# Stores moved to GpSimd's queue, a new reading order for PSUM banks, and a new order of work after the last image in a two-layer spectral kernel

## The chip, the cores and the metric

The kernel runs on one core of one Trainium2 chip. The metric is the device time of one execution in microseconds (us). A core has a matrix engine (TensorE, PE in the profile), a vector engine (VectorE, DVE), a scalar engine (ScalarE, ACT), a general engine (GpSimd, POOL) and a queue processor (SyncE, SP). TensorE writes its results to PSUM (eight banks), from which DVE and ACT read them. DMA transfers between main memory and the on-chip SBUF are issued in order from the queues of SP, ACT or POOL. All matrix work here is in 32-bit floating point.

## What is computed

The input `x` has 32 images of 32 channels, each channel a 128 x 128 matrix. Two layers follow each other, each on a normalised copy of its input (`_gn`: mean and variance over two channels):

```python
def _L0_conv_ref(A):                 # five Newton-Schulz steps towards the matrix square root
    normA = jnp.sqrt(jnp.sum(A2 * A2, axis=(1, 2)))
    Y = A2 / normA[:, None, None];  Z = I
    for _ in range(5):
        T = 0.5 * (3.0 * I - Z @ Y);  Y = Y @ T;  Z = T @ Z
    return Y * jnp.sqrt(normA)[:, None, None]
def _L1_conv_ref(x, weights1, weights2):       # a spectral layer on 2 x 32 x 32 modes
    x_dht = fftn(x).real
    top = einsum('bixy,ioxy->boxy', x_dht[:, :, :32, :32], weights1)
    bot = einsum('bixy,ioxy->boxy', x_dht[:, :, -32:, :32], weights2)
    return ifftn(out_dht).real                 # out_dht holds top and bot, zero elsewhere
x = x + _L0_conv_ref(_gn(x))
x = x + _L1_conv_ref(_gn(x), weights1, weights2)
```

## The kernel before

**Layer 0** works on groups of four channels, 8 groups to an image, 256 in all. `fetch` loads a group, `staged` scales it (four tensor_scalar on POOL at line 272, the sum with a scaled identity at line 291), and `newton` runs its chain of matrix products: TensorE multiplies (lines 248 and 254), DVE evicts some results (line 242) and ACT others (lines 234 and 236), POOL adds the identity in the middle of the chain (line 315), and DVE adds the result to the input tile `xt` (line 326). Four groups, the `lanes`, run interleaved, so that TensorE has another group's products while one waits for an eviction. Before an image's first group `prep` loads the whole image (`xs`, line 167) and takes its statistics on DVE (`bn_stats`, line 175).

**Between the layers** each finished group goes through `settle`: a copy of `xt` to main memory (`mid`, line 335), two sums of its column halves on POOL (`fold`, line 340), and `bn_stats` (line 344). After four groups `forward` transforms the folds (lines 358 to 370), and after eight `spectrum` makes the image's 64 x 32 modes (line 395), waits for the statistics (lines 147 to 155, 413 to 432), scales the modes and stores them (`xs`, line 449).

**Layer 1** works on sets of images, `GROUPS = (21, 8, 3)`. Once a set's last spectrum is stored, its products with the weights run (`wide_products`, line 492, for the first set; `small_products`, line 556, for the others), the results go to main memory (`od`), and then each image of the set goes through `inverse`. An inverse loads the products (`ob` or `or`, line 590) and the image's copy (`yt`, four tiles of 8 channels, line 601), transforms in two steps (lines 644 and 666), copies the sine half from PSUM to `d` on ACT (line 675), adds the cosine half from PSUM to `yt` on DVE (line 681), adds and subtracts `d` on POOL (`unfold`, line 619), and stores the result (`store`, line 609).

**The order.** The program is a set of generators. A round goes over the four lanes; queues named `preps`, `specs`, `posts`, `prods` and `backs` are stepped at fixed lanes, so that one round does one step of `posts` (folds and forwards), one of `specs` (spectra) and so on:

```python
if i == 2: step(specs)
if i == 3: step(posts)
if i == 0 or tail: step(prods)
if i == 0 and rounds % 5 or tail: step(backs)
```

`tail` is true when no group of layer 0 is left. Inverses of the second set (images 21 to 28) are left over then, and those of the third (29 to 31) can't begin, since image 31 is in that set. Once the tail has no `posts` left, the SBUF of layer 0 (`sets`) is freed and a pool `late` takes it: there go the weights of the last products (`wt_late`, 14 loads of 512 KB on POOL's queue, line 779) and three zeroed tiles (`xk_late`, line 776).

A scheduler fixes each engine's order when the program is built; the calls in `kept(...)` stay in program order among themselves on their queue. Every engine and every queue then works strictly in its order: an instruction that waits for a semaphore holds up everything behind it. The copies, loads of `xs` and `yt`, and stores of results all go through SP's queue, except that in the tail `store` uses ACT's.

Of the kernel before, what the change touches and what calls it, by code (L numbers as in the profile page):

```python
# [24 lines left out]
F32 = mybir.dt.float32  # L25
# [6 lines left out]
P = 128  # L32
B = 32
# [26 lines left out]
def conv_preact_kernel(  # L60
# [8 lines left out]
    nc = tc.nc  # L69
# [20 lines left out]
    mid = [dram.tile([P, C, P], F32, name=f"mid{b}", tag=f"mid{b}") for b in range(B)]  # L90
# [16 lines left out]
    inv = ctx.enter_context(tc.tile_pool(name="inv", bufs=1))  # L107
# [10 lines left out]
    tail = False  # L118

    def page(name):  # L120
        return modes.tile([P, 1024], F32, tag="page", name=name, bufs=3)

    def bank():
        return ps8.tile([P, 4, P], F32, tag="ps", name="ps")
# [33 lines left out]
    kept = tc.keep_in_program_order  # L158
# [173 lines left out]

    def settle(b, g, st, xt):

        kept(nc.sync.dma_start(out=mid[b][:, 4 * g : 4 * g + 4, :], in_=xt))
        if g % 2 == 0:
            folds[b, g // 2] = sets.tile([P, 8, P], F32, tag="fold", name=f"fold{b}_{g}", bufs=3)
        f = folds[b, g // 2][:, 4 * (g % 2) : 4 * (g % 2) + 4, :]
        for half, op in enumerate((ALU.add, ALU.subtract)):
            nc.gpsimd.tensor_tensor(  # L340
                f[:, :, 64 * half : 64 * half + 64], xt[:, :, 0:64], xt[:, :, 64:128], op
            )
        for j in range(4):
            nc.vector.bn_stats(st[:, 4 * g + j, :], xt[:, j, :])
        yield
# [110 lines left out]
    def wide_products(i):  # L456
# [26 lines left out]
        for step in range(2 * KK):  # L483
# [23 lines left out]
            if step + 2 < 2 * KK:  # L507
                load(step + 2)
        store(*done)
        yield  # L510

# [65 lines left out]
    yts = {}  # L577

    def load_products(b):
        if b < B and b not in obs:  # L580
            g, n = where[b]
            few = GROUPS[g] <= NB

            ob = page(f"or{b}") if few else inv.tile([P, 1024], F32, tag="ob", name=f"ob{b}", bufs=2)
            if few:
                src, dst = od[g][:, :, :, n, :].rearrange("k q l x -> (k q) l x"), "p (l x) -> p l x"
            else:
                src, dst = od[g][:, :, n, :].rearrange("k q x -> (k q) x"), "p (l x) -> p (l x)"
            for e in range(2):
                kept(nc.sync.dma_start(out=ob[64 * e : 64 * e + 64].rearrange(dst, l=4), in_=src))  # L590
            obs[b] = ob

    def load_input(b, e):

        if b >= B or (b, e) in yts:
            return
        yts[b, e] = []
        for i in range(2):
            o = 16 * e + 8 * i
            y = inv.tile([P, 8, P], F32, tag="yt", name=f"yt{b}_{o}", bufs=6)  # L600
            kept(nc.sync.dma_start(out=y, in_=mid[b][:, o : o + 8, :]))  # L601
            yts[b, e].append(y)

# [2 lines left out]
    def store():  # L606
        while stores:
            b, o, y = stores.pop(0)
            kept((nc.scalar if tail else nc.sync).dma_start(out=out[b, :, o : o + 8, :], in_=y))  # L609

    sums = []

    def unfold():

        while sums:
            b, o, y, d = sums.pop(0)
            for half, op in enumerate((ALU.subtract, ALU.add)):
                yh = y[:, :, 64 * half : 64 * half + 64]
                nc.gpsimd.tensor_tensor(yh, yh, d, op)  # L619
            stores.append((b, o, y))  # L620

    def inverse(b):


        more = where[b][1] < GROUPS[where[b][0]] - 1
        load_products(b)
        load_input(b, 0)
        yield
        ob = obs[b]
        if GROUPS[where[b][0]] <= NB:  # L630
            ob = inv.tile([P, 1024], F32, tag="ob", name=f"ob{b}", bufs=2)
            nc.scalar.copy(  # L632
                ob.rearrange("p (o t l) -> p o t l", t=8, l=4),
                obs[b].rearrange("p (l t o) -> p o t l", l=4, t=8),
            )
        ob = ob.rearrange("p (e j m) -> p e j m", e=2, j=4)
        if more:
            load_products(b + 1)

        pg = [bank() for _ in range(2)]  # L640
        for j in range(4):
            for e in range(2):
                rows = slice(64 * e, 64 * e + 64)
                nc.tensor.matmul(
                    pg[e][:, j, :], ob[rows, e, j, :], tab[rows, T_IH], start=True, stop=True
                )
        gts = []
        for e in range(2):
            gts.append(inv.tile([P, 4, P], F32, tag="gt", name=f"gt{b}_{e}", bufs=3))
            nc.scalar.copy(gts[e], pg[e])  # L650
        unfold()
        yield
        for e in range(2):
            store()

            py = [bank().rearrange("p j x -> p (j x)") for _ in range(4)]
            py = [p.rearrange("p (s c h) -> p s c h", s=2, h=64) for p in py]
            cos, sin = (slice(T_IW.start + P * i, T_IW.start + P * i + P) for i in range(2))
            for s, table, h, g in (
                (0, cos, slice(0, 64), slice(0, 64)),  # L660
                (1, sin, slice(1, 64), slice(65, 128)),
                (1, cos, slice(0, 1), slice(64, 65)),
            ):
                for i in range(4):
                    rows = slice(32 * i, 32 * i + 32)
                    nc.tensor.matmul(
                        py[i][:, s, :, h],
                        tab[rows, table],
                        gts[e][rows, :, g],
                        start=True,  # L670
                        stop=True,
                    )
            d = page(f"d{b}_{e}").rearrange("p (c h) -> p c h", h=64)
            for i in range(4):
                nc.scalar.copy(d[:, 4 * i : 4 * i + 4, :], py[i][:, 1])  # L675
            for i in range(2):
                for j in range(2):
                    y = yts[b, e][i][:, 4 * j : 4 * j + 4, :]
                    y = y.rearrange("p c (s h) -> p c s h", s=2)
                    half = py[2 * i + j][:, 0, :, None, :].to_broadcast([P, 4, 2, 64])  # L680
                    nc.vector.tensor_tensor(y, half, y, ALU.add)  # L681
                unfold()
                sums.append((b, 16 * e + 8 * i, yts[b, e][i], d[:, 8 * i : 8 * i + 8, :]))
                if not i:
                    yield
            if not e:
                load_input(b, 1)
            elif more:
                load_input(b + 1, 0)
            yield  # L690
        if not more:
            unfold()
            yield
            store()
# [3 lines left out]
    posts = []  # L698
    specs = []
# [3 lines left out]
    def step(queue):  # L703
        if queue and next(queue[0], queue) is queue:
            queue.pop(0)


    late = []
    late_xks, late_wts = [], []
# [6 lines left out]
    ended = {}  # L716
# [50 lines left out]
    rounds = 0  # L767
    while todo or any(lanes) or posts or specs or prods or backs:
        tail = not todo and not any(lanes)
        if tail and not posts and not late:  # L770

            phase.close()
            late.append(ctx.enter_context(tc.tile_pool(name="late", bufs=1)))
            for i in range(3):
                late_xks.append(late[0].tile([P, 4 * NB, 64], F32, name=f"xk{i}_late"))
                nc.gpsimd.memset(late_xks[-1], 0.0)
            for kk in range(2, KK):
                late_wts.append(late[0].tile([P, 2, 4, 4, C], F32, name=f"wt{kk}_late"))
                nc.gpsimd.dma_start(out=late_wts[-1], in_=wk[kk])
        for i in range(LANES):  # L780
            if lanes[i] is None and todo and rounds >= 3 * i:
                b, g = todo.pop(0)
                xt = ready[0][0]
                lanes[i] = (b, g, xt, newton(g, made[b][2], *ready.pop(0)))
                if stages:
                    stage()
            if lanes[i] is not None:
                b, g, xt, steps = lanes[i]
                if next(steps, lanes) is lanes:
                    lanes[i] = None  # L790
                    end(b, g, xt)
            if i == 1:
                step(preps)
            if i == 2:
                step(specs)
            if i == 3:
                step(posts)
            if i == 0 or tail:
                step(prods)
            if i == 0 and rounds % 5 or tail:  # L800
                step(backs)
        rounds += 1

# [63 lines left out]
```

## Time and profile before

Three runs took 3258.66, 3259.20 and 3259.95 us; the profiled execution has a span of 3256.9 us. Times below are counted from the span's start.

| stretch, us | what runs | PE busy | DVE busy | POOL busy | data moved |
|---|---|---|---|---|---|
| 100 to 1960 | layer 0 alone | 1841.35 of 1860.00 | 1361.42 | 940.20 | 98 GB/s |
| 1960 to 3105.6 | layer 0, with layer 1 of earlier images beside it | 1103.67 of 1145.60 | 806.60 | 724.57 | 214 GB/s |
| 3105.6 to 3256.9 | the tail: what is left of layer 1 | 60.91 of 151.30 | 36.43 | 73.76 | 267 GB/s |

A stretch in which PE is busy all the time can only get shorter by less matrix work; one in which it is idle has another cause for its length, and the chain of waits has to be followed there. The times at which the tail's stages begin:

| event in the tail | start, us |
|---|---|
| last `xt` added up (line 326), ends | 3105.6 |
| last forward's first matmul (line 358) | 3109.29 |
| last image's spectrum on PE (line 395) | 3141.35 |
| its store to main memory (line 449) | 3163.15 |
| first product of the third set (line 556) | 3173.65 |
| first `ob` copy of the third set's inverses (line 632) | 3208.77 |
| first result of image 29 issued for storing (line 609) | 3221.41 |
| end | 3256.9 |

### The profile page before, as it was taken

To read this page: it belongs to the slowest core of one execution; us is meant where nothing else is said; L and a number is where in the kernel's file an instruction comes from. 1 tells how busy PE (TensorE), PEld (TensorE's weight loads), DVE (VectorE), ACT (ScalarE), POOL (GpSimd) and SP (SyncE) were. 2 spreads that over 40 slices of the span, in tenths; PEclk is the share of its full clock that TensorE was granted. 3 is DMA by queue.
4 is the path that set the end of the run, shared out by engine and by line. 5 is a ranking of instruction groups with operands and counts; after the bars stand their busy time and mean duration, and the time that the engine had idled before them with its cause. 6 is when DMAs were issued, how large, how long until landed. Compare 5 with 4: busy or idle time off the path is not lost. (4 is left out here: it accounts for less than half of the span.)

```text
span 3256.9 us, 78280 instructions
## 1 busy us (share of the span) xinstructions
PE 3076.2 (94%) x30656; PEld 2944.7 (90%) x30656; DVE 2265.8 (70%) x6372; ACT 1457.9 (45%) x3068; POOL 1784.7 (55%) x2333
## 2 busy tenths in 40 slices
PE   6999999999999999999999999999999999999944
PEld 6999999999999999999999999899989898989933
DVE  5777777777777777777777776477777776756631
ACT  3444444444444444444444444444444444435522
POOL 4554545455454545444555554367667766746663
PEclk9999999999999999999999999999999999999966
DMA  3333333332233333333322336676666666686596
GB/s 121 98 104 98 101 101 102 95 97 93 88 102 101 102 101 98 104 98 95 95 90 93 101 98 194 210 223 208 227 218 196 208 224 220 215 263 191 186 319 208
DMA packets 271746, 479.37 MB, mean 147 GB/s; under 512 B 80656, under 2 KB 91408, under 8 KB 271376
## 3 DMA queue, kind: packets, MB, share of 16 engines
q1 hardware_dynamic: 191744, 318.61, 30.7%
q10 hardware_dynamic: 77616, 148.41, 14.1%
q0 software_dynamic: 2016, 7.34, 0.6%
q8 instruction: 242, 3.96, 0.5%
q14 instruction: 128, 1.05, 0.1%
HBM read 319.06 MB, written 155.19 MB: 146 GB/s over the span
## 5 line engine op out<-in xcount | busy, mean ns | idle before, releaser
L340 POOL TENSOR_TENSOR fold<-xt 128x256 f32<-128x256 f32 x512 | 362.6, 729 | 645.4 <-DVE xt L326 581.0
L291 POOL TENSOR_TENSOR r<-b,eye 128x512 f32<-128x512 f32 x256 | 326.6, 1276 | 609.1 <-issue 584.5
L248 PE MATMUL ps<-w,v 128*128 128x128 f32 x4096 | 548.1, 277 | 4.7 <-DVE w L242 3.2
L248 PE MATMUL ps<-y,q 128*128 128x128 f32 x4096 | 544.2, 276 | 1.2 <-ACT y L234 1.2
L248 PEld LDWEIGHTS ps<-w,v 128*128 128x128 f32 x4096 | 500.1, 193 | 7.8 <-DVE w L242 4.6
L248 PEld LDWEIGHTS ps<-y,q 128*128 128x128 f32 x4096 | 500.3, 193 | 2.1 <-ACT y L234 1.6
L234 ACT COPY y<-ps 128x512 f32<-128x512 f32 x512 | 299.5, 585 | 361.9 <-PE ps L248 361.7
L272 POOL TENSOR_SCALAR x<-xt,a_nm,a_sc 128x128 f32<-128x128 f32 x1024 | 448.3, 451 | 21.9 <-DVE a_n L204 20.1
L282 ACT ACTIVATE b<-b,a_off,a_scr 128x128 f32<-128x128 f32 x1024 | 422.3, 486 | 1.9 <-DMA b<-in_x 1.8
L619 POOL TENSOR_TENSOR yt<-yt,d 128x512 f32<-128x512 f32 x256 | 319.4, 1274 | 164.7 <-DVE yt L681 151.1
L242 DVE SCALAR_TENSOR_TENSOR w<-ps,r 128x512 f32<-128x512 f32 x512 | 347.3, 683 | 56.3 <-PE ps L254 53.5
L242 DVE SCALAR_TENSOR_TENSOR q<-ps,eye 128x512 f32<-128x512 f32 x512 | 348.9, 683 | 51.6 <-PE ps L248 43.2
L175 DVE BATCH_NORM_STATS2 a_st<-xs 128x6 f32<-128x128 f32 x1024 | 231.5, 280 | 216.8 <-DMA xs<-in_xt 215.8
L315 POOL TENSOR_TENSOR r<-mb,eye 128x512 f32<-128x512 f32 x256 | 325.7, 1272 | 23.1 <-ACT mb L236 23.1
L236 ACT ACTIVATE mb<-ps 128x512 f32<-128x512 f32 x256 | 153.1, 598 | 408.1 <-PE ps L254 407.0
L254 PE MATMUL ps<-ident,v 128*128 128x128 f32 x2048 | 312.3, 275 | 13.9 <-DVE v L242 13.3
L242 DVE SCALAR_TENSOR_TENSOR v<-ps,m 128x512 f32<-128x512 f32 x256 | 175.6, 686 | 213.1 <-PE ps L248 212.3
L326 DVE SCALAR_TENSOR_TENSOR xt<-ps,a_t_s,xt 128x128 f32<-128x128 f32 x1024 | 289.2, 342 | 49.5 <-PE ps L248 47.9
L248 PE MATMUL ps<-m,q 128*128 128x128 f32 x2048 | 283.6, 282 | 31.7 <-DVE q L242 30.8
L248 PEld LDWEIGHTS ps<-m,q 128*128 128x128 f32 x2048 | 250.2, 193 | 46.1 <-DVE q L242 31.8
L248 PE MATMUL ps<-y,t 128*128 128x128 f32 x2048 | 280.2, 280 | 5.1 <-DVE t L242 4.7
L242 DVE SCALAR_TENSOR_TENSOR v<-ps,x 128x512 f32<-128x512 f32 x256 | 175.7, 686 | 154.9 <-PE ps L248 154.5
(118 smaller groups left out, 5212.1 us busy)
## 6 DMA issues: line engine op xcount, KB each, us to landing
b<-in_x ACTq DMA_DIRECT2D x256, 256.0 KB, 2.9
xt<-in_xt ACTq DMA_DIRECT2D x256, 256.0 KB, 3.2
xs<-in_xt SPq DMA_DIRECT2D x256, 256.0 KB, 3.5
mid<-xt SPq DMA_DIRECT2D x256, 256.0 KB, 2.0
yt<-mid SPq DMA_DIRECT2D x128, 512.0 KB, 6.4
out<-yt SPq DMA_DIRECT2D x101, 512.0 KB, 4.9
out<-yt ACTq DMA_DIRECT2D x27, 512.0 KB, 5.6
ob<-od SPq DMA_DIRECT2D x42, 256.0 KB, 4.2
```

The costliest lines, as they stand in the source:

```text
L175: nc.vector.bn_stats(st[:, 4 * i + c, :], tiles[i][:, c, :])
L234: nc.scalar.copy(t, ps)
L242: nc.vector.scalar_tensor_tensor(s, ps, f, t, ALU.mult, ALU.add)
L248: nc.tensor.matmul(ps[:, j, :], lhsT[:, j, :], rhs[:, j, :], start=True, stop=True)
L254: nc.tensor.transpose(ps[:, j, :], t[:, j, :], ident)
L272: nc.gpsimd.tensor_scalar(m[:, j, :], xt[:, j, :], nm[:, c // 2 : c // 2 + 1], sc[:, c : c + 1], ALU.add, ALU.mult,)
L282: nc.scalar.activation(mb[:, j, :], mb[:, j, :], AF.Identity, bias=off[:, c : c + 1], scale=scr[:, c : c + 1],)
L291: nc.gpsimd.tensor_tensor(r, mb, eye, ALU.add)
L315: nc.gpsimd.tensor_tensor(r, mb, eye, ALU.add)
L326: nc.vector.scalar_tensor_tensor(xt[:, j, :], ps[:, j, :], sn[:, c : c + 1], xt[:, j, :], ALU.mult, ALU.add)
L340: nc.gpsimd.tensor_tensor(f[:, :, 64 * half : 64 * half + 64], xt[:, :, 0:64], xt[:, :, 64:128], op)
L619: nc.gpsimd.tensor_tensor(yh, yh, d, op)
```

## The change

The change does seven things. (1) `settle` issues the copy `mid` from POOL's queue, behind the fold, rather than from SP's. (2) Outside the tail `store` issues results from POOL's queue, behind the sums that make them, so that SP's queue, which carries the loads, needn't wait for groups and sums to finish. (3) In `inverse` ACT copies from the two banks that DVE isn't reading: banks 2 and 3 while DVE reads 0 and 1, then the other way round. (4) In the tail the second half of each pair's sums goes to DVE rather than POOL. (5) Once `late` exists, every second `yt` tile comes from it (four more buffers), so that more loads can be in flight. (6) The three tiles are zeroed by DVE rather than POOL. (7) The order of work: near the end of layer 0 (more than 26 images finished) `backs` is stepped in every round, not in four of five; in the tail `specs` and `posts` are stepped at every lane, and `backs` only once both are empty, so that the last image's transforms aren't put behind left-over inverses.

```diff
     def settle(b, g, st, xt):
-        kept(nc.sync.dma_start(out=mid[b][:, 4 * g : 4 * g + 4, :], in_=xt))
...
+        kept(nc.gpsimd.dma_start(out=mid[b][:, 4 * g : 4 * g + 4, :], in_=xt))
         for j in range(4):
             nc.vector.bn_stats(st[:, 4 * g + j, :], xt[:, j, :])
...
-            y = inv.tile([P, 8, P], F32, tag="yt", name=f"yt{b}_{o}", bufs=6)
+            turn = len(yts) + i
+            if late and turn % 2:
+                y = late[0].tile([P, 8, P], F32, tag="yt_late", name=f"yt{b}_{o}", bufs=4)
+            else:
+                y = inv.tile([P, 8, P], F32, tag="yt", name=f"yt{b}_{o}", bufs=6)
             kept(nc.sync.dma_start(out=y, in_=mid[b][:, o : o + 8, :]))
...
-            kept((nc.scalar if tail else nc.sync).dma_start(out=out[b, :, o : o + 8, :], in_=y))
+            kept((nc.scalar if tail else nc.gpsimd).dma_start(out=out[b, :, o : o + 8, :], in_=y))
...
+            engine = nc.vector if tail and o % 16 else nc.gpsimd
             for half, op in enumerate((ALU.subtract, ALU.add)):
                 yh = y[:, :, 64 * half : 64 * half + 64]
-                nc.gpsimd.tensor_tensor(yh, yh, d, op)
+                engine.tensor_tensor(yh, yh, d, op)
...
-            for i in range(4):
-                nc.scalar.copy(d[:, 4 * i : 4 * i + 4, :], py[i][:, 1])
             for i in range(2):
+
+                for j in range(2):
+                    n = 2 * (1 - i) + j
+                    nc.scalar.copy(d[:, 4 * n : 4 * n + 4, :], py[n][:, 1])
                 for j in range(2):
...
-                nc.gpsimd.memset(late_xks[-1], 0.0)
+                nc.vector.memset(late_xks[-1], 0.0)
...
-            if i == 2:
+            if i == 2 or tail:
                 step(specs)
-            if i == 3:
+            if i == 3 or tail:
                 step(posts)
             if i == 0 or tail:
                 step(prods)
-            if i == 0 and rounds % 5 or tail:
+            if i == 0 and (rounds % 5 or len(ended) > B - 6) or tail and not (posts or specs):
                 step(backs)
```

## The prediction

> **What bounds the kernel now.** First I read the busy shares by stretch (columns: length, then busy us of PE, its weight loads, DVE, ACT and POOL, each with its count; granted PE clock, DMA share, GB/s).
>
> ```profile
> 100.00:1960.00 1860.00, 1841.35 (x16585) 1783.42 (x16586) 1361.42 (x3971) 843.54 (x1745) 940.20 (x1330) 1.00 0.31 98
> 1960.00:3105.60 1145.60, 1103.67 (x12067) 1042.33 (x12066) 806.60 (x2135) 542.76 (x1173) 724.57 (x868) 0.99 0.66 214
> 3105.60:3256.90 151.30, 60.91 (x1434) 51.38 (x1434) 36.43 (x68) 37.73 (x80) 73.76 (x68) 0.60 0.77 267
> ```
>
> Up to 3105.6 PE has only 18.7 us of gaps in the first stretch and 41.9 us in the second. The change removes no matrix work, so these 61 us are all that it can win there. In the tail PE is busy for 60.9 of 151.3 us at 0.60 of its clock: here the order of work sets the time. Next, PE's waits in the second stretch and at the tail's start (engine, line, what it waited for, us in total, times, longest).
>
> ```profile
> PE ps L248 <- DVE q L242: 16.9, 17, 3.7
> PE ps L254 <- DVE v L242: 9.5, 7, 2.3
> ```
>
> ```profile
> PE ps L420 <- DVE b_qr L415: 15.0, 1, 15.0
> PE ps L644 <- ACT ob L632: 7.8, 2, 7.6
> ```
>
> In the main part PE waits for evictions on a DVE that was held up by something ahead in its order. In the tail a single wait of 15.0 us belongs to the last image's statistics. The timeline there shows why the spectrum is late:
>
> ```profile
> 3140.60 2.48 DVE L681 TENSOR_TENSOR yt<-ps,yt 128x512 f32<-128x512 f32 x4 [6.92 <-ACT d L675]
> 3150.40 1.29 DVE L681 TENSOR_TENSOR yt<-ps,yt 128x512 f32<-128x512 f32 x2 [7.31 <-DMA yt<-mid]
> 3154.00 1.29 DVE L681 TENSOR_TENSOR yt<-ps,yt 128x512 f32<-128x512 f32 x2 [2.32 <-DMA yt<-mid]
> 3155.21 0.16 DVE L149 COPY b_nm<-ps 128x16 f32<-128x16 f32 x1
> ```
>
> The last image's statistics (line 149) stand behind three left-over inverses, which wait for loads. So the store of the last spectrum comes at 3163.15, 57.5 us after the last `xt`. From there the chain is serial: 10.5 us to the first product (3173.65), 28.0 us of products (to 3201.6), 7.2 us until `ob` (3208.8), and 48.1 us for three inverses. In those the chain of waits goes from POOL's sums through a result's store to the load that wants its buffer:
>
> ```profile
> 3234.75 1.29 POOL yt L619
> 3236.04 0.02 issue
> 3236.06 5.57 DMA out<-yt
> ...
> 3241.75 5.41 DMA yt<-mid
> ```
>
> **What the Trainium skill says.** "SBUF — State Buffer", section "SBUF: two separate sides": DVE and GpSimd share a port pair under an exclusive lock; a DVE instruction with two SBUF inputs is blocked for the whole of a GpSimd instruction that reads SBUF. The trace agrees: a DVE operation on one column (line 132, median 0.82 us in this group, 0.16 at the least) took 4.45 us while POOL ran four sums and one more, and PE then waited 2.3 us.
>
> ```profile
> 2509.63 4.45 DVE L132 TENSOR_TENSOR b_r_q<-b_r_q,b_v 128x1 f32<-128x1 f32 x1
> ```
>
> "DMA: Bandwidth & Descriptors", section "Issuing engines are not separate DMA queues": all queues end on the same 16 DMA engines, so another queue only saves issue time. The trace doesn't contradict it; what the move can win is a queue's waiting. "VectorE: DVE Perf Modes", section "Zero memsets can be issued as uint32 (trn2)": a memset takes a cycle per element. With the 0.96 GHz of its Specifications I estimate 2.13 us for 2,048 elements; POOL's took 1.80.
>
> **The change, part by part.** *Copies and stores through POOL* (256 copies, 108 stores outside the tail in the new order). The nearest row:
>
> ```profile
> L779 POOL DMA_DIRECT2D wt_late<-in_wk x14: 527/529/721, 3128.0 to 3157.4; - x14
> ```
>
> So 364 x 0.53 = 193 us more on POOL, about 0.8 us per 12 us group; POOL was busy 51% in the first and 63% in the second stretch, so it goes to some 55% and 73% (155 and 96 groups, the stores all in the second). At the low end this is free; at the high end an issue in front of `r` (line 315) or a blocked DVE operation reaches PE. Nothing waits newly for long: a copy is issued behind a fold that waits for the same `xt`; behind it on POOL stand `r` and the next group's scaling, and DVE's `w` waits for `r`. On the other side SP waited 1458 us in all for `xt` at line 335, with loads of `xs` and `yt` behind it; these now go early, and DVE's 66 us of waits for `xs` after 1960 shrink. *PSUM order*: DVE's waits for `d` (26 us between 1960 and 3105.6, from its waits) mostly go. Of the 41.9 us of PE gaps I take 8 us as won, between 15 lost (POOL later, lock met more often) and 30 won. The first stretch I leave at nothing, since its 18.7 us lie in slips below 2 us.
>
> *Inverses ahead.* In the new order all of image 26 and half of 27 come before the last product of layer 0; before, only 26's first step did. PE pays 3 x 1.26 us (line 666) + 1.16 us (line 644) = 4.9 us, in a stretch where it has no room. So the last `xt` ends at 3105.6 + 4.9 - 8 = 3102.5.
>
> *Last image first.* From there, by the order on the engines: fold and forward 3.7 us as before; forward, copy, transpose, copies, spectrum and the mean's product, with 27's last 12 matmuls between, some 12 us. On DVE in front of and among the statistics now stand three memsets (3 x 2.13 = 6.4 us), four additions (4 x 0.68) and four sums (each between 0.66, as line 681 takes, and 1.9, behind one sum of POOL's). The first memset waits for the last copy to land (POOL's fold 1.4, issue 0.5, 2 to 5 us), so to about +8. I take +16 for the mean, +23 for line 415, then 0.8 on PE and 3.7 us as before (3159.45 to 3163.15): the store at +28, where before it was +57.5. This is the main gain, 29.5 us; its ends are +22 and +38.
>
> *After that*: 10.5 us to the first product (loads of 12 MB, late weights most of them, run beside; at the 372 GB/s reached at 3120 to 3140 that is 32 us, just done). Products 28.0 us plus image 28's inverse between them, at the tail's speed 2.1 + 2 x 2.2 = 6.5 us. Three us I add for pages of `d`, of which the products now want some. Then 7.2 us: `ob` at +83.
>
> *The last three inverses.* Ten `yt` buffers rather than six take most loads off the stores. Sums: POOL 4 x 1.27 = 5.1 us per image rather than 9.8; DVE 8 x 0.68 + 4 sums, 8 to 10 us under the lock. An image took 12.2 us (first stores 3221.4, 3233.6, 3245.8); I take 9. First store 12.7 us after `ob` as before, two images more 18, the third's rest 7, landing 4: 42 us, 6 less. The end: +125.
>
> Sum: 3102.5 + 125 = 3227.5; the runs' median stood 2.3 us over the span, so **3230 us**.
>
> **The rivals.** *The main part gains too* (the SP waits and the PSUM order were the cause of most gaps; 30 won rather than 8): 3208. For it: DVE held by `xs` and `d`; against: the lock stays. *The tail is bound by transfers*: in it 40.4 MB moved; without 1.5 images (4.2 MB each) and at 350 GB/s that is 97 us, which fits, but weights, stores and loads are all due before the products, and loads of `xs` behind them would cost 10 to 20 us: 3246. *POOL becomes the bound*: were a sixth of its 193 us of issues to reach PE through `r` or the lock, that would be 32 us, and the 8 us aren't won: 3230 + 8 + 32 = 3270, slower. For it: the 4.45 us above; against: no wait for `r` in PE's or DVE's list, and PE nearly full with POOL at 63%.
>
> **How the numbers follow.** Forecast 0.56, main part too 0.17, transfers 0.18, POOL 0.09. I let the range begin a little below the first rival, at 3206, and end at 3251, beyond the transfers' case; the POOL case and tails, near 0.15, stay out. Faster by over 0.2% (below 3252.7): 0.56 + 0.17 + 0.16 = 0.89; within: 0.03; slower: 0.08.
>
> **What would show it.** Right: the last spectrum's store about 28 us after the last `xt`, few SP waits at line 449 and none at 335, about 49 us rather than 55 from the last product to the end. Wrong: PE busy for less of the second stretch and new waits for `r`; a main part longer by more than 10 us; or first products later than 45 us after the last `xt`, with the DMA engines full.

## The result, and the profile after

The changed kernel takes 3332.43 us (median; 3327.21 to 3336.35), the kernel before took 3259.57 us beside it: a ratio of **1.0219, 95% interval 1.0202 to 1.0237**. It is 2.2% slower, where 3230 us were predicted. The profiled execution after has a span of 3325.4 us, 68.5 us more than before.

The tail does what was predicted, and the loss lies ahead of it. The last `xt` ends at 3199.1 instead of 3105.6 us: the main part is 93.5 us longer. From there to the end it takes 126.3 us instead of 151.3, 25.0 us less. The busy shares by stretch, with the same columns as in the prediction (length; PE, weight loads, DVE, ACT, POOL, each with its count; granted PE clock; DMA share; GB/s). First the tail of the changed kernel:

```profile
3199.10:3325.40 126.30, 47.72 (x1346) 41.29 (x1346) 57.68 (x83) 29.87 (x66) 40.02 (x37) 0.62 0.78 270
```

For the main part a cut at a fixed time would mix images, so I cut at the last `xt` of image 20 and of image 31, in the kernel before and in the changed one:

```profile
1924.70:3105.20 1180.50, 1138.66 (x12390) 1076.09 (x12390) 831.81 (x2207) 558.89 (x1207) 742.04 (x893) 0.99 0.65 210
```

```profile
1940.70:3198.70 1258.00, 1166.63 (x12472) 1097.99 (x12474) 871.43 (x2215) 571.02 (x1221) 856.25 (x1097) 0.97 0.63 202
```

So 16.0 us are lost up to image 20 (1940.7 against 1924.7) and 77.5 us in the rest. (Single executions differ: three other kernels below that have the copies on POOL's queue reach that point 20 to 27 us after the kernel before, and one whose program is that of the kernel before up to there, 6 us after it.) Of these 77.5 us, 49.5 are gaps of PE (1258.0 - 1166.6 = 91.4 against 41.8), and 28.0 are time in which PE counts as busy: the trace has 82 matmuls more there, and the granted clock is lower, 0.97 for 0.99. The gaps stand in the waits after image 20 (1960 to the last `xt`; columns as before):

```profile
PE ps L254 <- DVE v L242: 24.8, 17, 5.4
PE ps L248 <- DVE q L242: 21.9, 14, 6.1
```

As before, PE waits for evictions on DVE, but for 24.8 rather than 9.5 us for `v` and 21.9 rather than 16.9 for `q`, and now for up to 6.1 us at a time. What holds DVE itself is in its own list:

```profile
DVE a_st L175 <- DMA xs<-in_xt: 80.8, 35, 6.7
```

These are the statistics of the next image, waiting for loads of `xs`: 80.8 us where it was 66.3, and up to 6.7 us rather than 4.0. (Before image 20 these waits became fewer: 104.5 us between 100 and 1920 us, where it was 131.6.) I took every PE gap of 1 us or more in the two second stretches and looked at which instruction of DVE had the longest wait just ahead of it. Before: 16 gaps, 29.3 us, of which 12 gaps (23.0 us) behind line 175. After: 31 gaps, 78.6 us, of which 14 (43.2 us) behind line 175, 4 (10.0 us) behind `yt` at line 688, 3 (5.3 us) behind line 242, and 10 (20.1 us, before 3.7 us) in which DVE had no wait of 1 us. The split depends on how far back one looks: within 3 us, two gaps fewer count to line 175 and three more to the last kind. In about half of those ten a small operation was held up by POOL, as this one was:

```profile
3132.61 5.01 DVE L151 TENSOR_TENSOR b_d<-b_st,b_nm 128x64 f32<-128x64 f32 x1
```

The queue that the change was to free is not free. SP's waits, 100 to 1960 us, in the changed kernel:

```profile
SPq L449 <- DMA b<-in_x: 797.7, 21, 93.9
SPq L449 <- DVE xt L326: 737.9, 20, 37.1
```

The waits at the copy (line 335) are gone, and SP stands at the next thing in its order instead, the store of the spectrum, for 1535.6 us of 1860, where it stood 204.3 us before (the releaser behind the first line is inferred; the store waits for its spectrum). The loads of `xs` come behind it. One image on SP's queue, before and after (start, length, instruction):

```profile
1072.94 0.37 SPq L449 DMA_DIRECT2D xs<-spec  x1
1073.98 0.32 SPq L335 DMA_DIRECT2D mid<-xt  x1
1074.35 10.21 SPq L167 DMA_DIRECT2D xs<-in_xt  x5
1086.03 0.33 SPq L335 DMA_DIRECT2D mid<-xt  x1
1086.41 2.69 SPq L167 DMA_DIRECT2D xs<-in_xt  x2
1096.13 0.33 SPq L335 DMA_DIRECT2D mid<-xt  x1
1096.55 0.38 SPq L167 DMA_DIRECT2D xs<-in_xt  x1
```

```profile
1083.86 0.38 SPq L449 DMA_DIRECT2D xs<-spec  x1
1084.29 18.37 SPq L167 DMA_DIRECT2D xs<-in_xt  x8
```

In both kernels the first load follows the spectrum's store within 1.5 us. The first load goes no earlier. What changed is that the eight loads come in one bunch, and the scheduler, which had these loads free of copies, placed their statistics more closely together on DVE: in images 1 to 20 they take 17.4 us from the first group of four to the last (median), where they took 21.8. With two buffers each load also waits for the statistics of the one two places before it. So evictions on DVE still stand behind waits for loads; whether these cost PE time depends on the place of each wait in DVE's order as much as on their sum.

### The profile page after: what moved, and what is told of

The parts are those of the page before. It is cut to its first block, busy times and chain, and to the rows that moved or that the text cites. A ratio compares the mean times of both kernels' runs of the same rounds, so it can differ in the third digit from the quotient of the medians.

```text
span 3325.4 us, 78416 instructions
## 1 busy us (share of the span) xinstructions
PE 3098.5 (93%) x30656; PEld 2959.7 (89%) x30656; DVE 2333.8 (70%) x6395; ACT 1462.7 (44%) x3068; POOL 1952.9 (59%) x2674
## 3 DMA queue, kind: packets, MB, share of 16 engines
q1 hardware_dynamic: 140336, 198.52, 20.1%
q14 instruction: 129, 1.06, 0.1%
## 4 chain that ended last, share of the span: by engine, by line
PE 68%; DVE 14%; DMA 13%; issue 2%; ACT 1%; POOL 1%; SPq 1%; DVEq 0%; ACTq 0%; POOLq 0%
PE ps L248 52%; DMA xs<-in_xt 10%; PE ps L254 8%; DVE a_st L175 3%; DVE xt L326 2%; DVE w L242 2%; DVE q L242 1%; PE ps L671 1%; DVE yt L688 1%; PE ps L358 1%; PE ps L556 1%; DMA or<-od 1%; PE ps L492 1%; PE ps L395 1%; ACT spec L437 1%
## 5 line engine op out<-in xcount | busy, mean ns | idle before, releaser
L624 POOL TENSOR_TENSOR yt<-yt,d 128x512 f32<-128x512 f32 x236 | 300.0, 1294 | 149.2 <-ACT d L683 138.3
L248 PE MATMUL ps<-m,q 128*128 128x128 f32 x2048 | 287.9, 284 | 28.6 <-DVE q L242 25.6
```

What stands on the lines that cost most here:

```text
L248: nc.tensor.matmul(ps[:, j, :], lhsT[:, j, :], rhs[:, j, :], start=True, stop=True)
L624: engine.tensor_tensor(yh, yh, d, op)
```

## The experiments

Eighteen kernels were run. They undo or add parts of the change, most of them one at a time, first on the side of the changed kernel ("after"), then on the side of the kernel before. All ratios are against the kernel before on the same chip.

### Which part of the change costs it

**PSUM order undone in the changed kernel.**

```diff
-                for j in range(2):
-                    n = 2 * (1 - i) + j
-                    nc.scalar.copy(d[:, 4 * n : 4 * n + 4, :], py[n][:, 1])
...
+            for i in range(4):
+                nc.scalar.copy(d[:, 4 * i : 4 * i + 4, :], py[i][:, 1])
```

> The changed kernel with one part undone: ACT copies all four sine halves before DVE starts, as before. Three theories for the 93 us by which the last xt is late (3198.7 against 3105.2 us). BANKS: the new reading order makes ACT's copies of the second pair wait for DVE (54 us of ACT's waits between 2300 and 2900 us), and behind them on ACT stand the evictions of layer 0; then undoing it gives back most of the 70 us that images 23 to 28 lost: last xt near 3135, time near 3268. STORES: results stored late from POOL's queue hold the buffers, and SP waits for them with the image loads behind (362 us of waits of SP for stores between 2300 and 2900); then the time stays above 3310. COPIES: POOL's issues of the copies cost layer 0; then it stays above 3310 too.

Measured 1.0206 [1.0176, 1.0235]: no difference from 1.0219 that these runs can tell. The reading order is not the cause.

**Stores back on SyncE, copies back on SyncE, both back** (three kernels, each from the changed one).

```diff
-            kept((nc.scalar if tail else nc.gpsimd).dma_start(out=out[b, :, o : o + 8, :], in_=y))
+            kept((nc.scalar if tail else nc.sync).dma_start(out=out[b, :, o : o + 8, :], in_=y))
```

```diff
+        kept(nc.sync.dma_start(out=mid[b][:, 4 * g : 4 * g + 4, :], in_=xt))
...
-        kept(nc.gpsimd.dma_start(out=mid[b][:, 4 * g : 4 * g + 4, :], in_=xt))
```

> The changed kernel with one part undone: results outside the tail are stored from SP's queue as before; the copies stay on POOL's. STORES: images 23 to 28 take about 110 us each again rather than 120 to 128, time near 3270. BANKS or COPIES: images 23 to 28 stay at 120 us or more, time above 3310. A mixture of STORES and BANKS: half, near 3295.

> The changed kernel with one part undone: the copies of finished groups go through SP's queue ahead of the fold as before; the stores stay on POOL's. COPIES, as far as layer 0 alone goes: the 6 us lost by image 0 and the 10 us that grow by image 20 come back, time near 3315. If the copies' 0.57 us each on POOL are also the cause of the 70 us in images 23 to 28: near 3250. If early image loads (free of the copies) are what packs DVE's order, the same.

> The changed kernel with copies and stores both back on SP's queue; reading order of the banks and the order of work stay changed. If the reading order is harmless by itself (undoing it in the changed kernel moved nothing): the time of the kernel with only the tail's parts, 3253. If its waits of ACT for DVE cost in the main part: later by 10 us or more, 3265.

Measured 1.0155 [1.0122, 1.0188] with the stores back, 1.0124 [1.0095, 1.0154] with the copies back, 1.0013 [0.9997, 1.0029] with both. With the stores back it took 3314 us, where the theory of the stores had 3270. With the copies back it took 3304, between the two expectations, and the loss up to image 20 falls to 3.8 us, no more than executions differ by. So nearly the whole loss hangs on these two moves together.

**The two moves alone, on the kernel before** (the same two diffs, the other way round).

> The kernel before with one part of the change alone: results outside the tail are stored from POOL's queue. STORES as the main cause: images 23 to 28 take 115 us or more each rather than 108, last xt near 3150, time near 3300. Only together with the copies (POOL's queue full of both): last xt at 3105 to 3120, time within 15 us of before.

> The kernel before with one part alone: the copies go through POOL's queue behind the fold. COPIES: 6 us lost by image 0, 10 to 20 by image 20 as in the changed kernel, and in images 23 to 28 some 5 us per image more, time near 3295. If the copies hurt only where layer 1 runs beside: nothing lost by image 20, 3285. If they hurt only together with the stores: 3275.

Measured 1.0079 [1.0055, 1.0102] for the stores and 1.0139 [1.0088, 1.0191] for the copies, some 26 and 45 us, the first between its two expectations, the second beyond the 3295 us expected. TensorE's order of instructions is that of the kernel before in both, so no other order of the matrix work explains them. With the stores on Pool, SP's waits at the loads of `yt` for a store to land (line 601) rise from 36.6 to 165.0 us, and DVE's for `xs`, whose loads stand behind in SP's order, from 66.3 to 88.6 us (image 20 to the last `xt`). With the copies on Pool these waits did not grow. In images 1 to 20 DVE waited 110.2 us for `xs`, where it was 128.8, and after image 20 65.1, where it was 66.3. PE's gaps grew all the same, from 18.7 to 28.6 us and from 41.8 to 63.0. In images 1 to 20 every gap of PE of 0.3 us or more, 24 gaps with 21.8 us, stands behind such a wait; in the kernel before 8 of 19 did (8.4 of 15.1 us). Most of them are waits for `t`, about once in an image (140 to 1940 us; before, `t` is not in this list):

```profile
PE ps L248 <- DVE t L242: 18.3, 19, 1.7
```

So the sum of the waits for loads didn't grow with the copies. In images 1 to 20 some of them came to stand in front of an eviction that PE needs at once; after image 20 no run shows what the copies added.

**The tail alone, with and without the inverses in every round.** First the changed kernel with copies, stores and PSUM order as before; then also

```diff
-            if i == 0 and (rounds % 5 or len(ended) > B - 6) or tail and not (posts or specs):
+            if i == 0 and rounds % 5 or tail and not (posts or specs):
```

> The changed kernel with copies, stores and reading order all undone; what is left is the new order of work at the end, the four more yt buffers, the zeroing and half of the tail's sums on DVE. All three theories: the main part is that of before plus some 5 us for the inverses moved ahead, the tail that of the changed kernel (126 us from the last xt): 3110 + 126 + 2 = 3238, faster than before by 0.6%. If the tail's gain hangs on stores from POOL: its end is late by 10 us or more, 3250.

> Only the tail's parts (copies, stores and reading order as before), and of them not the stepping of inverses in every round after image 26: one inverse and a half more are left over for the tail. If that stepping is what costs images 26 to 28 some 17 us (112, 113 and 117 us rather than 110, 104 and 108): last xt near 3108, and the tail as long as 126 plus what the left-over inverses add, 5 to 15 us: 3245. If the loss in these images comes from elsewhere: last xt still near 3125, time 3260.

Measured 0.9969 [0.9959, 0.9979] and 0.9959 [0.9950, 0.9968]. Both beat the kernel before, by less than the 3238 and 3245 us expected (3253 and 3252). The early inverses win nothing in all: the last `xt` starts at 3131.0 us with them and at 3114.8 without, and both profiled spans are 3256.0 us. In these two executions they cost 16.2 us of the main part and give the same 16 us back in the tail.

### What of a transfer on Pool costs the time

**A small transfer, a fill and a reading operation on Pool**, each added once per group behind the fold of the kernel before, with the copies left on SyncE.

```diff
+        kept(nc.gpsimd.dma_start(out=spare[8 * b + g], in_=xt[:, 0, 0:4]))
```

```diff
+        kept(nc.gpsimd.memset(void, 0.0))
```

```diff
+        kept(nc.gpsimd.tensor_scalar(void, xt.rearrange("p j x -> p (j x)")[:, 0:128], 1.0, 0.0, ALU.mult, ALU.add))
```

> The kernel before, in which Pool issues one more small transfer (128x4 of xt, to a place that nobody reads) behind each fold, at the place where the change puts a set's copy; the copies stay on SyncE. 256 issues more on Pool, and nothing else: TensorE, VectorE and ScalarE have their instructions in the same order as before. If Pool's issues cost the time by themselves (held VectorE operations or a late Pool): most of the 53 us that the copies on Pool cost, 3295 to 3315 us, ratio 1.010 to 1.015, VectorE's small operations held up by some 10 us more in the first 21 images. If it is SyncE's freedom (earlier loads of xs, another order of the statistics on VectorE): no change, 3255 to 3268 us, ratio 0.999 to 1.001. Both in half: about 1.007.

> The kernel before with a fill (128x400 zeros, an estimated 0.43 us from the fills of 1,024 and 2,048 elements) on Pool behind each fold, in the place of the small transfer. It takes Pool's time as an issue does, but reads no SBUF. If Pool's occupation is what costs: 256 x 0.43 = 110 us of Pool, four fifths of an issue's time, so some 0.8 of what the small transfers cost (1.008 to 1.012 if those cost the 53 us). If it is an issue's hold on VectorE: about nothing, ratio 0.999 to 1.003.

> The kernel before with a 128x128 operation on Pool that reads xt and writes a spare tile (0.44 us, as the scaling of line 272 takes) behind each fold. As long as the fill, but it reads SBUF. If what costs is the lock between VectorE and Pool, this costs more than the fill by the time for which VectorE is held: 256 more operations, ratio 1.008 to 1.015 against the fill's 1.000 to 1.003. If Pool's occupation costs: the same as the fill. If neither: 1.000 for both.

Measured 1.0291 [1.0272, 1.0309] for the transfer, 1.0011 [1.0001, 1.0020] for the fill and 1.0010 [1.0001, 1.0018] for the reading operation. The transfer cost twice the most that was expected of it. The groups on POOL of the first two:

```profile
L342 POOL DMA_DIRECT2D spare<-xt x256 | 143.9, 562 | 2.7 <-issue 2.7
```

```profile
L342 POOL MEMSET void<- 128x400 f32 x256 | 110.4, 431 | 0.0
```

The fill takes 110.4 us of POOL, three quarters of the transfers' 143.9, and costs a tenth of a per cent. So POOL's time is not what is short; the theory that POOL becomes the bound falls. The hold on DVE is there, and it goes with the transfers: I added up by how much DVE's operations of less than 0.3 us exceed their undisturbed length (the tenth percentile over these kernels). In images 1 to 20 that is 31 us in the kernel before, 28 with the fill, 24 with the reading operation, and 48 with the small transfers or with the copies alone on Pool. The operations that got longer (line 195: 0.70 us rather than 0.53 at the median) run beside Pool's sums and scalings at lines 315 and 272, not beside the transfers themselves. (The reading operation was shorter than expected, 0.30 us.) What the small transfers did besides is seen elsewhere: the loads of `xs` land later. From 100 to 1920 us they took 3.3 us from issue to landing in the kernel before (median), and with the small transfers:

```profile
xs<-in_xt SPq DMA_DIRECT2D x156, 256.0 KB, 4.0
```

And DVE, on which every order is the same as before, waited 190.4 us for them rather than 131.6:

```profile
DVE a_st L175 <- DMA xs<-in_xt: 190.4, 101, 4.2
```

This is not how the copies cost time: with the copies alone on Pool the loads of `xs` landed after 3.3 us there, as before. And the small transfer was run on Pool's queue alone; no run shows what it costs on SyncE's or ScalarE's.

**The loads of `xs` on ScalarE's queue**, in the kernel before; nothing on Pool.

```diff
-            kept(nc.sync.dma_start(out=t, in_=xt_in[b, :, 4 * i : 4 * i + 4, :]))
+            kept(nc.scalar.dma_start(out=t, in_=xt_in[b, :, 4 * i : 4 * i + 4, :]))
```

> The kernel before with the loads of xs, which the statistics of the next image read, issued by ScalarE rather than SyncE: they no longer stand behind copies that wait for xt. No issue is added to Pool; the statistics move on VectorE much as in the change, and TensorE's order is as before. If early loads and the moved statistics cost the time: as with the copies on Pool, 3295 to 3315 us, ratio 1.010 to 1.015. If Pool's issues cost it: 0.998 to 1.003 (256 issues on ScalarE are near its gaps; where one waits for a buffer, its evictions come later, a few us).

Measured **0.9930** [0.9915, 0.9945]. One theory expected a loss as large as that of the copies, the other no change; it wins 22 us. DVE's waits for `xs` up to 1920 us, 131.6 us in 104 waits before, are nearly gone:

```profile
DVE a_st L175 <- DMA xs<-in_xt: 9.6, 23, 0.9
```

PE's gaps from image 1 to image 20 fall from 18.7 to 0.8 us, and every image there takes 88.2 us, where it took 88.4 to 90.9. The gaps of the first stretch went with the waits for `xs` in DVE's order. (The edit lets the scheduler move the statistics on DVE too; what the earlier loads and what the new places did is not told apart.) After image 20 it wins nothing: 1181.5 us to the last `xt`, where it was 1180.5, and PE's gaps are 42.4 us, where they were 41.8.

### How much of the loss goes with those loads

**The same edit on top of copies on Pool, of stores on Pool, of the whole change, and of the tail alone (without early inverses)**, and last on top of the small transfers. For the stores and the small transfers all orders on TensorE, VectorE and ScalarE are those of the kernel at 0.9930.

> The kernel before with the sets' copies issued by Pool behind the fold, as in the change, and the loads of xs issued by ScalarE. TensorE's order is that of before; VectorE's and ScalarE's are those of the kernel with the xs loads alone on ScalarE up to the second stretch. If what the copies cost is VectorE waiting for xs loads in front of TensorE's evictions: 3240 to 3255 us, ratio 0.993 to 0.997, and TensorE's gaps in the first 21 images stay near 1 us. If Pool's issues cost it in another way (held VectorE operations, a late Pool): 53 to 75 us over the kernel with the xs loads alone on ScalarE, 3295 to 3317 us, 1.009 to 1.016.

> The kernel before with the results' stores issued by Pool, as in the change, and the loads of xs issued by ScalarE; all orders on TensorE, VectorE and ScalarE are those of the kernel with the xs loads alone on ScalarE. If SyncE, held at loads of yt by the later stores, kept the xs loads back: the 26 us that the stores cost mostly go, 3242 to 3252 us, 0.993 to 0.996. If Pool's issues or the late yt cost it: 3262 to 3275 us, 1.000 to 1.003.

> The changed kernel with the loads of xs issued by ScalarE, nothing else. If the waits for xs are the cause of its longer main part: 3240 to 3265 us, ratio 0.993 to 1.001, with TensorE's gaps in the first 21 images near 1 us and in the rest near the 42 us of before. If Pool's 364 issues cost otherwise: only the 22 us that the same edit wins on the kernel before, 3305 to 3315 us, 1.014 to 1.017.

> The tail of the change without the inverses in every round (copies, stores and the order of the PSUM readers as before), 3252 us by itself, with the loads of xs issued by ScalarE. The two gains lie in different stretches: 13 us and 21.7 us, so 3230 to 3234 us, ratio 0.989. If they share something (ScalarE's issues late in front of the tail), less: 3238 us, 0.992.

> The small transfer per group on Pool again (256 issues, 128x4 of xt, copies on SyncE), now with the loads of xs issued by ScalarE. All orders on TensorE, VectorE and ScalarE are those of the kernel with the xs loads alone on ScalarE, 0.993 of before. With the loads on SyncE the small transfers cost 93 us. If they cost it only through xs loads that landed late: at most 8 us over 0.993, so 3240 to 3250 us, ratio 0.993 to 0.9955, and the first 21 images take 88.2 us each. If Pool's issues also hold work in the second stretch, where Pool is busiest (24 us were left for the copies there): 3256 to 3275 us, 0.998 to 1.004.

| kernel | `xs` loads on SyncE | on ScalarE |
|---|---|---|
| before | 1 | 0.9930 [0.9915, 0.9945] |
| copies on Pool | 1.0139 | 1.0000 [0.9992, 1.0008] |
| stores on Pool | 1.0079 | 0.9961 [0.9949, 0.9973] |
| small transfers on Pool | 1.0291 | 1.0066 [1.0054, 1.0078] |
| the whole change | 1.0219 | 1.0049 [1.0036, 1.0063] |
| tail alone, no early inverses | 0.9959 | **0.9908** [0.9894, 0.9922] |

Down each column the difference from the first row is what an edit costs. The copies cost 1.4% with the loads on SyncE and 0.7% without, the stores 0.8 and 0.3%, the small transfers 2.9 and 1.4%, the change 2.2 and 1.2%. **About half of the loss goes with the loads.** Against what was expected, stores and tail came out as in the first theory, the copies and the whole change lie between the two, and the small transfers' 1.0066 is above both. The loss goes where it was expected: with the copies on Pool and the loads on ScalarE, images 0 to 20 lose 3.8 us against the loads alone on ScalarE (1904.9 against 1901.1), and each of nearly all of them takes 88.2 us. What is left, 23.8 of 27.6 us, is lost after image 20.

There late loads still hold PE, and a long gap costs more than its length. From the timeline of the kernel with copies on Pool and loads on ScalarE, DVE and then PE, with the wait in front in brackets:

```profile
2546.48 0.87 DVE L175 BATCH_NORM_STATS2 a_st<-xs 128x6 f32<-128x128 f32 x4 [8.37 <-DMA xs<-in_xt]
2547.39 0.24 DVE L144 TENSOR_REDUCE a_ms<-a_st 128x16 f32<-128x64 f32 x1
2547.54 1.28 DVE L681 TENSOR_TENSOR yt<-ps,yt 128x512 f32<-128x512 f32 x2
2548.74 0.68 DVE L242 SCALAR_TENSOR_TENSOR w<-ps,r 128x512 f32<-128x512 f32 x1
```

```profile
2549.57 2.05 PE L248 MATMUL ps<-w,v 128*128 128x128 f32 x8 [7.45 <-DVE w L242]
2551.40 1.92 PE L248 MATMUL ps<-m,q 128*128 128x128 f32 x8
2553.11 1.92 PE L248 MATMUL ps<-y,q 128*128 128x128 f32 x8
2554.82 1.21 PE L248 MATMUL ps<-m,mb 128*128 128x128 f32 x8
2555.86 1.06 PE L248 MATMUL ps<-x,q 128*128 128x128 f32 x8
```

The load was issued at 2536.05 and landed some 10 us later, among loads of `yt` and stores. DVE stands in front of it for 8.37 us; the eviction `w` behind it is late, and PE waits 7.45 us. Then PE runs at half speed, with a granted clock of 0.50 from 2549 to 2555: eight matmuls take 2.05, 1.92 and 1.92 us instead of 1.06. The gap costs 7.5 us and the slow stretch after it some 2.7 more (0.99 + 0.86 + 0.86). The Trainium skill ("TensorE: Matmul & The Clock Gate", section "Part 1: The HAM clock gate") says that the array falls to half its clock after an idle window of some 3.4 us and comes back after a busy one. This trace agrees on the half; the way back took about 5 us here.

**A third buffer for `xs`**, in the changed kernel with the loads on ScalarE. Room comes from one buffer rather than two for the next image's statistics.

```diff
+    stp = ctx.enter_context(tc.tile_pool(name="stp", bufs=3))
...
+        st = small.tile([P, C, 6], F32, tag="a_st", name=f"a_st{b}", bufs=1)
...
+        load(1); load(2)
...
+            if i + 3 < C // 4:
+                load(i + 3)
```

> The changed kernel with the loads of xs on ScalarE (1.0049) and three buffers for them rather than two, loaded three ahead (room for it comes from one rather than two buffers for the next image's statistics, of which one is in use at a time). If loads that land late with VectorE standing in front of them are most of what is left in the second stretch: 3245 to 3262 us, ratio 0.996 to 1.001, VectorE's waits for xs after image 20 from 80 us to under 30, TensorE's gaps there from 82 us to 55 or less. If what is left comes from Pool's issues, the stores or the order of the inverses: 3270 to 3282 us, 1.003 to 1.006.

Measured 0.9991 [0.9981, 1.0001] where two buffers gave 1.0049: 0.6%, 16 to 19 us, for a buffer. The ratio lies in the range of the first expectation, but the waits and gaps behind it do not. DVE's waits for `xs` after 1905 us go from 80.3 us to

```profile
DVE a_st L175 <- DMA xs<-in_xt: 53.9, 26, 5.8
```

and not under 30, and PE's gaps there from 82.6 to 74.6 us, not to 55. So late loads are a cause in the second stretch too, but not the whole of it. The third buffer was not run on the kernel before, so part of the 0.6% may be a gain that any version would have.

## Why the prediction was wrong, point by point

**The sum for the main part failed.** It read 3105.6 + 4.9 - 8 = 3102.5; measured, 3199.1. Its own sign of being wrong, a main part longer by more than 10 us, came true. Three terms of it were wrong.

*"364 x 0.53 = 193 us more on POOL ... at the low end this is free", 8 us won, the first stretch at nothing.* The price of an issue was right: the rows of the changed kernel say 566 and 547 ns.

```profile
L342 POOL DMA_DIRECT2D mid<-xt x256 | 145.0, 566 | 2.8 <-issue 2.8
L613 POOL DMA_DIRECT2D out<-yt x108 | 58.9, 547 | 1.8 <-POOL yt L624 1.5 <-DMA xt<-in_xt 0.3
```

POOL's time was also as free as said, by the fill. But I priced the issues and not what the moves do to the loads and to their place in DVE's order. Alone, the copies cost 45 us and the stores 26.

*"These now go early, and DVE's 66 us of waits for `xs` after 1960 shrink."* This is the step that failed. I had SP's waits at line 335 and didn't ask what stands next in SP's order: the store at line 449, which waits for an image's spectrum. The loads were behind it before and after; after 1960 the waits for `xs` grew to 80.8 us. The prediction's own sign for the move, few waits at 449 and none at 335, had its second half come true and its first fail: SP stood 1535.6 us at line 449. That the loads' queue matters is shown: about half of the loss goes when they leave SP's queue. That this step alone turned the sign is not, since the other half stays.

*4.9 us for the inverses moved ahead.* The direction was right and the size was not: 16.2 us by the two tail-only kernels. Of these, 8.1 are PE busy (1147.2 against 1139.1 us after image 20) and 6.4 more gaps; the 1.7 before image 20 are no more than two executions differ by.

**The 18.7 us of the first stretch** were put down to "slips below 2 us" and left alone. They went together, and an edit of one line wins them: 0.9930. The list of DVE's waits had 131.6 us for `xs` there, the largest entry that was not a wait for PE, and the prediction doesn't read it for that stretch.

**The PSUM order** was to take away most of DVE's 26 us of waits for `d`, with PE's gaps following. The waits went: 25.9 us before, 0.2 in the changed kernel (image 20 to the last `xt`). PE's gaps didn't follow. ACT's copies now wait for DVE instead, 62.5 us in 55 waits at line 683 in the changed kernel, a wait that the prediction didn't count. Undoing the order in the change did nothing measurable. With copies and stores on SyncE the kernel with the new order stands at 1.0013 [0.9997, 1.0029] and the one with the old at 0.9969 [0.9959, 0.9979], so there it costs time. ACT waits 49.2 us for DVE in the first of these two; whether that is the cause was not tried.

**The tail was right** in its mechanism and in its sum, with some luck in between. Counted from the end of the last `xt`: spectrum's store +24.0 (predicted +28), first product +38.3 (+38.5), `ob` +82.7 (+83), end +126.3 (+125). The store was 4 us early and the step from it to the first product 14.3 us rather than 10.5, so two errors cancel there. The events, from the timeline of the changed kernel:

```profile
3223.15 0.37 SPq L449 DMA_DIRECT2D xs<-spec  x1
...
3237.42 1.98 PE L556 MATMUL ps<-plain,diag 128*32 128x32 f32 x121 [16.18 <-DMA diag<-xs]
...
3281.81 1.92 ACT L637 COPY ob<-or 128x1024 f32<-128x1024 f32 x1 [7.49 <-DMA or<-od]
...
3283.78 2.08 PE L649 MATMUL ps<-tab,ob 64*128 64x128 f32 x16 [10.12 <-ACT ob L637]
```

The fills were a little cheaper than the 2.13 us estimated from the Trainium skill ("VectorE: DVE Perf Modes"): 1.76 us each. From the last product to the end it took 51.7 us, 3.6 less than before, where 49 had been expected.

**The rivals.** The one that came nearest in sign, POOL as the bound at 3270, was too small by 62 us and had only part of the mechanism. Its lock is there: counted as above, small operations of DVE were held up for some 17 us more in images 1 to 20 and some 37 us more after (31 and 24 us before, 48 and 61 after). With the copies on Pool and the loads on ScalarE the first of these is as large (48 us) and costs PE next to nothing: its gaps in images 1 to 20 are 1.8 us. What the second costs is open. The rival in which the main part gains 22 us more named SP's waits and the PSUM order. Moving the loads off SP does win 22 us, but before image 20, where the prediction had left the gaps at nothing, and this change doesn't move them; the PSUM order won nothing. "DMA: Bandwidth & Descriptors" says that another queue saves issue time only; the same copies on Pool's queue rather than SyncE's cost 0.7% even with the loads on ScalarE (1.0000 against 0.9930), so here the move was a loss.

**What stays open.** With the loads on ScalarE and three buffers, the changed kernel's main part still ends 58 us later than that of the kernel with the loads alone on ScalarE (3140.7 against 3082.6 us). Some 16 of these are the early inverses. For the other 42, held operations of DVE, the later stores and the waits at line 688 are all seen in the trace, and no run separates them. By parts of the change, with two buffers and the loads on ScalarE, the copies alone end the main part 27.6 us later and the stores alone 9.2, of 71.9 for the whole. The small transfers cost 1.4% even with the loads off SyncE; in these two kernels the orders on TensorE, VectorE and ScalarE are the same. Half of the 42.3 us stand before image 20, where images take some 89 us rather than 88.2 and DVE's waits for `xs` are 33.5 rather than 8.7 us. Loads land 0.5 to 0.6 us later after image 20 (`xs` 5.4 against 4.8, `xt` 4.9 against 4.4), and DVE's small operations are held some 13 us more on either side of it. Which of the two does it was not tried, nor why a transfer of 2 KB delays other loads.

## What to carry to other kernels

When a wait is taken out of an in-order queue, read the next instruction in that queue: it may wait for something later still, and the loads behind it then come all at once. Before moving transfers to free a queue, look which loads an engine stands in front of in its own order; here moving those loads (0.9930), not the copies and stores around them, was the gain, and with the new tail it makes 0.9908. And price a change in a full stretch by what it does to the waits for loads and to their place in front of evictions, not by the busy time of an engine with room.

## What the runs showed of the hardware that was not expected

- After a gap of 7.45 us TensorE ran for some 5 us at half speed (2.05 us for eight matmuls that take 1.06). The prediction had counted gaps by their length alone. In this case the wait cost a third more than its length; over the second stretch of the changed kernel the granted clock was 0.97, where it was 0.99 before.
- 256 transfers of 2 KB on Pool's queue, 0.56 us of Pool each, cost 2.9% of the time, 93 us, while 256 fills of 0.43 us in the same place cost 0.1%. DVE's small operations were held 17 us more in images 1 to 20 with the transfers, and no more with the fills. The transfers were not tried on another queue.
- A fill of 2,048 elements took 1.76 us on VectorE and 1.80 on Pool.
